# Attention inputs read during layer 3, an earlier overflow flag, and a re-timed attention plan

## The chip, the cores and the metric

The kernel runs on one core of one Trainium2 chip. The metric is the device time of one execution in microseconds. The engines are named as the profile names them: PE (TensorE), DVE (VectorE), ACT (ScalarE), POOL (GpSimd) and SP (SyncE, which here only issues DMAs).

## The reference, cut to what matters

x holds 32 images of 1024 channels and 14 x 14 pixels. Two residual layers follow each other. `_amm` stands for scores against 16 centroids per group, a softmax over the 16, and a product with a table; `_gn` and `_bn` are group and batch norms.

```
x = x + L0(_gn(x)):                     # three table layers
    out = relu(bn1(_amm(x, c1, lut1)))              # 1024 -> 256
    out = relu(bn2(_amm(extract3x3(out), c2, lut2)))  # 256 -> 256
    out = bn3(_amm(out, c3, lut3))                    # 256 -> 1024
    return relu(out + identity)
x = x + L1(_gn(x)):                     # linear attention, 16 heads of 64
    q = elu(Wq x[:512] + bq) + 1;  k = elu(Wk x[512:] + bk) + 1
    qr, kr = rope(q), rope(k);  v = x
    z  = 1 / (q . mean_n(k) + 1e-6)
    kv = s*s * sum_n kr v;   attn = (qr kv) * z
    lepe = depthwise_conv3x3(x, lepe_w) + lepe_b
    return attn + lepe
```

All sums run in float32. bn3 needs the mean and variance of all tokens, so attention can begin only when layer 3 is done.

## The kernel before, in words

Layers 1 to 3 are in `layers` (L419). Layers 1 and 2 go through 16 pairs of images, 8 units a pair (`units`, L543): a unit's scores, exponentials, softmax (DVE transposes, sums, reciprocal, and one POOL product) and the product with its table block on PE, the last one some units behind the first. Layer 3 (L850 to L930) goes through 14 chunks `k` of 448 tokens. For a chunk, PE makes 8 blocks `m` of 128 channels, each out of 8 products with `luts` (L909); ACT copies a block to `o` (L917), DVE takes its statistics (L918), and SP stores `o` to the scratch `o3d` in DRAM (L924). `o` has two buffers. In between, the scores of the next chunk are made (L874, L881) and its softmax. After the last chunk `add_up` sums the softmax denominators, and `bn_final` (L320) turns statistics into scale `sc3` and shift `bi3`.

The exponentials are taken without a maximum. Denominators that overflow are found by a flag: three sums are compared with 1e36 (L940), reduced, summed over partitions by a small PE product (L943), written as an integer `bad` (L945) and loaded into a register of each engine (L946). The branch at L947 repeats the three layers in an exact form if the flag is set, which it is not in the profile.

Attention (from L954) first loads its weights `wk` and `wq` into the eight `lut` buffers (L243), biases, masks and tables (L974 to L998), and derives small tables on DVE (L986 to L1016). The order of everything after that is written by `Plan.write`: each piece of work has an engine, a rank and a weight; the planner runs the pieces in a model, taking on each engine the ready one with the lowest rank, and the instructions are then issued in that order, engine by engine.[...] Buffers belong to slots; a slot's ring is taken in turn.

`pair(p, t)` gives the pieces of one pair of images, `t` being 80 p. For each half of the channels (h=1 for keys, h=0 for queries): `load` takes x and two thirds of `o3d`; `front` scales x into a bank `w` (ACT, L1124), adds layer 0's result and the residual (DVE, L1133, L1138) and takes statistics (L1143); `group_norm` averages on PE (L1165) and ends on POOL; `normalise` writes the padded images `y` (ACT, L1218). `channels` makes 8 key and 8 query products (PE, L1250; ACT, L1259 and L1262; DVE, L1271 or L1267). `rope` turns them on POOL (L1291 to L1298). `tokens` transposes on PE (L1309), `products` makes kv (L1346, L1355), `normalisers` makes z (PE L1397, DVE L1406 and the reciprocal L1407). `normalise_q` spreads z over partitions with a PE product by `hsel` (L1418), an ACT copy `zb` (L1424) and a POOL product (L1421). `attend` puts a channel pair's sums into two banks `pa` (PE, L1438), and `lepe` adds eight taps of the 3 x 3 convolution there one by one (DVE, L1455; the middle tap is in the residual's scale) and then adds `pa` to x (L1469). `store` writes x out (L1478).

Of the kernel before, what the change touches and what calls it, by code (L numbers as in the profile page):

```python
# [10 lines left out]
F32 = mybir.dt.float32  # L11
# [30 lines left out]
class Slot:  # L42


    def __init__(self, pool, make):
        self.pool, self.make, self.ap, self.left = pool, make, None, 0
# [5 lines left out]
class Plan:  # L52
# [9 lines left out]
    def __init__(self, bufs):  # L62
        self.pieces, self.last, self.read = [], {}, {}
        self.ring = {n: [None] * k for n, k in bufs.items()}
# [19 lines left out]
    def write(self):  # L84
# [9 lines left out]
        nexts = {n: 0 for n in self.ring}  # L94
# [7 lines left out]
        def roomy(slots):  # L102
            take = {}
            for s in slots:
                if s.ap is None:
                    ring = self.ring[s.pool]
                    k = take.get(s.pool, nexts[s.pool])
                    old = ring[k % len(ring)]
                    if old is not None and old.left:
                        return False  # L110
                    take[s.pool] = k + 1
            return True

        while events:
            now, _, done = heapq.heappop(events)
            if done is not None:
# [4 lines left out]
                for s in self.pieces[done][5]:  # L121
                    s.left -= 1
            if events and events[0][0] <= now:
                continue
            for e in engines:
# [17 lines left out]
                for s in slots:  # L143
                    if s.ap is None:
                        ring = self.ring[s.pool]
                        ring[nexts[s.pool] % len(ring)] = s
                        nexts[s.pool] += 1
                        s.ap = s.make()
# [12 lines left out]
def conv_preact_kernel(ctx: ExitStack, tc: tile.TileContext, a: dict, out: bass.AP):  # L161
# [78 lines left out]
    def load_lut(name, shape, src, b):  # L240

        t = wts.tile(shape, F32, tag=f"lut{b}", name=f"{name}_{b}")
        nc.sync.dma_start(t, src(b))  # L243
        return t

    def load_luts(name, shape, src):
        return [load_lut(name, shape, src, b) for b in range(8)]
# [72 lines left out]
    def bn_final(pool, stats, i, hs, sc, bi):  # L320
# [4 lines left out]
        mv = pool.tile([P, n, 2], F32, tag=f"mv{hs[0]}", name=f"mv{i}")  # L325
        for k, h in enumerate(hs):
            nc.vector.bn_aggr(mv[:, k, :], stats[:, h].rearrange("p m s -> p (m s)"))
# [80 lines left out]
    lut_rows = lambda t: lambda b: a[t][b * 512 : (b + 1) * 512].rearrange("(s q) w -> q s w", q=P)  # L408
# [5 lines left out]

    sc3 = cp.tile([P, CT], F32, tag="sc3", name="sc3")
# [3 lines left out]
    def layers(exact, sums):  # L419
# [107 lines left out]

        def add_up(layer, n):
# [1088 lines left out]
```

## Time and profile before

| quantity | value |
|---|---|
| time, median of 3 runs | 3925.6 us (3922.6 to 3926.0) |
| the profiled execution | 3921.2 us |
| its span | 3919.2 us |
| PE, DVE, POOL, ACT busy | 95%, 78%, 57%, 42% of the span |
| layer 3's last product ends | 2657.7 us |
| attention's first key product starts | 2712.5 us |
| last pair's first key product starts | 3793.0 us |

The profile is one execution on the chip, and its times count from the start of the span. A row names the line, the engine, the operation and what it writes and reads; in brackets stands how long the engine was idle before, and what ended that. Busy shares say little by themselves here, since layers, passage and attention have different limits; the times of three places are set beside the page in the table.

### The profile page before, as it was taken

Reading aid. Unit: us, or ns where it says so; the run is one execution under the profiler, and the core shown is the slowest. Engines: PE = TensorE matmul, PEld = TensorE weight load, DVE = VectorE, ACT = ScalarE, POOL = GpSimd, SP = SyncE. Lnnn points to the kernel's source line nnn. Section 1 sums busy time; section 2 is a strip of 40 time slices with the busy share of each in tenths; the row PEclk is TensorE's granted clock in tenths of the full one; section 3 lists DMA queues with packets and bytes.
Section 4 is the critical chain, followed back from the end, with each engine's and each line's share of the span. In section 5 each row is a group of like instructions: output and inputs, shape, how many; then the busy total and the mean of one; then the engine's idle time right before and its main releaser. Section 6 shows DMA issues by size and latency. Waiting matters only on the chain. (4 is left out here: it accounts for less than half of the span.)

```text
span 3919.2 us, 45921 instructions
## 1 busy us (share of the span) xinstructions
PE 3741.2 (95%) x16475; PEld 2097.3 (54%) x16475; DVE 3054.1 (78%) x4395; ACT 1664.6 (42%) x3797; POOL 2226.9 (57%) x1248
## 2 busy tenths in 40 slices
PE   8999999999999999999999999994999999999995
PEld 5555555544555455554444444442666666666664
DVE  8999999978888888888533333323799999999997
ACT  4555555533333333333222211213756666666661
POOL 7999999964444444444211111103877777777773
PEclk9999999999999999999999999997999999999997
DMA  3111111024333333432011110114122222222111
GB/s 114 34 34 33 34 33 32 2 74 104 83 69 87 69 83 69 97 73 60 32 38 38 38 38 19 38 38 135 42 67 62 71 71 63 67 71 75 55 54 34
DMA packets 209028, 228.13 MB, mean 58 GB/s; under 512 B 23888, under 2 KB 206672, under 8 KB 208792
## 3 DMA queue, kind: packets, MB, share of 16 engines
q1 hardware_dynamic: 208216, 224.96, 21.4%
q8 instruction: 133, 2.18, 0.2%
q14 instruction: 103, 0.84, 0.1%
q10 hardware_dynamic: 576, 0.15, 0.0%
HBM read 151.51 MB, written 73.55 MB: 57 GB/s over the span
## 5 line engine op out<-in xcount | busy, mean ns | idle before, releaser
L525 POOL TENSOR_TENSOR t<-t,r 128x1664 f32<-128x1664 f32 (+1 forms) x284 | 1064.2, 3747 | 1188.8 <-DVE r L524 1153.1
L558 PE MATMUL po<-t,lut 128*128 128x392 f32 x4096 | 1418.4, 500 | 0.5 <-POOL t L525 0.5
L558 PEld LDWEIGHTS po<-t,lut 128*128 128x128 f32 x4096 | 760.0, 190 | 627.0 <-issue 124.7
L487 ACT ACTIVATE t<-sc,cbias 128x392 f32<-128x392 f32 (+1 forms) x1136 | 579.8, 593 | 1034.8 <-PE sc L823 646.9
L1250 PE MATMUL mm<-y,qk 128*128 128x392 f32 x2048 | 727.1, 507 | 4.1 <-POOL xbi L1192 4.1
L909 PE MATMUL po<-t,lut 128*128 128x448 f32 x1792 | 680.3, 540 | 0.0
L499 DVE STREAM_TRANSPOSE tt<-t 128x1664 f32<-128x1664 f32 (+1 forms) x284 | 544.3, 1917 | 168.5 <-ACT t L487 168.5
L1455 DVE SCALAR_TENSOR_TENSOR pa<-y,lepe_w,pa 128x406 f32<-128x406 f32 x1024 | 607.1, 638 | 10.5 <-PE pa L1438 9.2
L524 DVE STREAM_TRANSPOSE r<-rc 128x1664 f32<-128x1664 f32 (+1 forms) x284 | 546.6, 1925 | 21.3 <-DVE rc L518 0.9
L1250 PEld LDWEIGHTS mm<-y,qk 128*128 128x128 f32 x2048 | 386.5, 194 | 283.9 <-issue 32.8
L909 PEld LDWEIGHTS po<-t,lut 128*128 128x128 f32 x1792 | 338.4, 190 | 339.9 <-issue 339.6
L918 DVE BATCH_NORM_STATS2 stats<-o 128x6 f32<-128x448 f32 x112 | 69.0, 617 | 488.4 <-ACT o L917 488.4
L516 DVE TENSOR_REDUCE sm<-tt 128x104 f32<-128x832 f32 (+2 forms) x284 | 423.1, 1490 | 5.4
L502 POOL TENSOR_TENSOR tt<-tt 128x832 f32<-128x832 f32 x128 | 248.1, 1938 | 7.8 <-DVE tt L499 7.8
L917 ACT COPY o<-po 128x448 f32<-128x448 f32 x112 | 59.0, 528 | 419.6 <-PE po L909 375.5
L518 DVE RECIPROCAL rc<-sm 128x104 f32<-128x104 f32 (+1 forms) x284 | 229.5, 808 | 9.8
L814 PE MATMUL sc<-patch,cw 64*128 64x392 f32 x1024 | 211.1, 520 | 4.7 <-DMA patch<-h1d 3.2
L1291 POOL TENSOR_TENSOR kr<-k,cosq 128x784 f32<-128x784 f32 x64 | 104.0, 1625 | 129.8 <-DVE k L1271 100.6
L1421 POOL TENSOR_TENSOR qr<-qr,zb 128x784 f32<-128x784 f32 x64 | 116.1, 1845 | 103.0 <-ACT zb L1424 103.0
L526 ACT ACTIVATE sm<-sm 128x104 f32<-128x104 f32 (+1 forms) x284 | 86.2, 304 | 174.6 <-DVE rc L518 174.6
L1124 ACT ACTIVATE w<-x,tb,gn_a 128x196 f32<-128x196 f32 x256 | 133.3, 521 | 58.5 <-DMA x<-in_x_dram 33.9
L814 PEld LDWEIGHTS sc<-patch,cw 64*128 64x128 f32 x1024 | 90.5, 186 | 116.5 <-issue 73.4
(156 smaller groups left out, 3844.6 us busy)
## 6 DMA issues: line engine op xcount, KB each, us to landing
patch<-h1d SPq DMA_DIRECT2D x248, 162.8 KB
x<-in_x_dram SPq DMA_DIRECT2D x32, 784.0 KB
o3d<-o SPq DMA_DIRECT2D x14, 1792.0 KB
x<-in_x_dram SPq DMA_DIRECT2D x64, 392.0 KB
o3q<-o3d SPq DMA_DIRECT2D x64, 392.0 KB
out_dram<-x SPq DMA_DIRECT2D x64, 392.0 KB
h1d<-pad SPq DMA_DIRECT2D x96, 225.0 KB
patch<-h1d SPq DMA_DIRECT2D x124, 108.5 KB
```

Source lines behind the costliest of these rows:

```text
L487: nc.scalar.activation(t[:, j, : sc.shape[1]], sc, AF.Identity if exact else AF.Exp, bias=bias[:, j : j + 1],)
L499: nc.vector.transpose(tt, tf)
L502: nc.gpsimd.tensor_tensor(tv[:, :, :8], tv[:, :, :8], tv[:, :, 8:], ALU.add)
L516: nc.vector.tensor_reduce(sm, tv, AX.X, ALU.add)
L518: nc.vector.reciprocal(rc, sm)
L524: nc.vector.transpose(r, bc(rc, 2, KC))
L525: nc.gpsimd.tensor_tensor(tf, tf, r, ALU.mult)
L558: nc.tensor.matmul(po[h], luts[b][:, j, h * P : (h + 1) * P], ts[u % len(ts)][:, j, :N2], start=(b == 0 and j == 0), stop=(b == 7 and j == 3),
L814: nc.tensor.matmul(sc, w8[r, 8 * h + 4 * (j // 2) + g], grid(pbuf[n % NPB][r, j // 2, g]), start=True, stop=False,)
L909: nc.tensor.matmul(po, luts[g][:, m * P : (m + 1) * P], t3[h][:, g % 4, :], start=(g == 0), stop=(g == 7),)
L1250: nc.tensor.matmul(pv(), w[kt][:, m0 : m0 + P], ywin(p, first + kt), start=(kt == 0), stop=(kt == 3),)
L1455: nc.vector.scalar_tensor_tensor(acc, neighbours(p, c, 15 * (k // 3 - 1) + k % 3 - 1), lw[:, c, k : k + 1], acc, ALU.mult, ALU.add,)
```

## The change

In the order of the program:

- The planner's buffers are made once, and a slot takes any free buffer of its kind instead of the next one of a ring. The eight table buffers are one set of tiles for all layers.
- A pool of its own holds attention's inputs. In layer 3, chunk 1 issues their loads (biases, masks, tables, x of the first pair), chunk 2 the loads of the first pair's `o3d` for the key half, chunk 3 derives the small tables. The weights are issued behind the last store of layer 3, ahead of the branch.
- The flag is formed and loaded into registers ahead of chunk 13's products. The aggregates of layer 3 are taken block by block in that chunk.
- Only borders of `y` and gaps of `kr` are set to zero.
- For the first pair, x and the key half's `o3d` are there already, and odd channels of `front` use a `pa` bank.
- For all pairs but the last, z is stored to the DRAM scratch `zd` and read back by four DMAs that repeat four rows over 128 partitions (`keep`, `spread`). The last pair keeps the PE product.
- Of each channel of the key half, one tap leaves DVE: ACT scales the shifted image into `side`, POOL adds it to x. In the last pair three taps of every channel go this way.
- In the last pair the five other taps of six channels are PE products with a diagonal matrix that ACT makes in `wk`'s buffers; they open the bank, and `attend` adds to it. The last two channels keep five taps on DVE.
- All ranks are a table `due`, with other values, and some pieces have `held` and `room` as further dependencies.

Cut to its core (rank table and renamed slots shortened):

```diff
-    def __init__(self, bufs):
+    def __init__(self, tiles):
         self.pieces, self.last, self.read = [], {}, {}
-        self.ring = {n: [None] * k for n, k in bufs.items()}
+        self.free = {n: list(ts) for n, ts in tiles.items()}
...
-            take = {}
-            for s in slots:
-                if s.ap is None:
-                    ring = self.ring[s.pool]
-                    k = take.get(s.pool, nexts[s.pool])
-                    old = ring[k % len(ring)]
-                    if old is not None and old.left:
-                        return False
-                    take[s.pool] = k + 1
-            return True
+            take = [s.pool for s in slots if s.ap is None]
+            return all(take.count(n) <= len(self.free[n]) for n in take)
...
+                    if s.left == 0:
+                        self.free[s.pool].append(s.ap)
...
-    def load_lut(name, shape, src, b):
-        t = wts.tile(shape, F32, tag=f"lut{b}", name=f"{name}_{b}")
-        nc.sync.dma_start(t, src(b))
-        return t
-    def load_luts(name, shape, src):
-        return [load_lut(name, shape, src, b) for b in range(8)]
...
+    def load_lut(b, src):
+        v = weights[b]
+        if len(src.shape) == 3:
+            v = v.rearrange("p (s w) -> p s w", s=src.shape[1])
+        nc.sync.dma_start(v, src)
+        return v
...
+    def bn_sum(mv, stats, h):
+        nc.vector.bn_aggr(mv, stats[:, h].rearrange("p m s -> p (m s)"))
...
+    def attention_inputs(stack):
+        def loads(_):
+            pool = stack.enter_context(tc.tile_pool(name="pre", bufs=1, side="right"))
+            def tile_(name, shape):
+                given[name] = pool.tile(shape, F32, tag=name, name=name)
+                return given[name]
+            for n, k in (("qb", a["qb"]), ("kb", a["kb"].rearrange("o (r j p) -> p (o r) j", p=P, r=2))):
+                nc.sync.dma_start(tile_(n, [P, 2, 4]), k)
+                tile_(n + "u", [P, 2, 4])
+                tile_(n + "d", [P, 2, 4])
+            for n, shape in (("lepe_w", [P, CT, 9]), ("lepe_b", [P, CT]), ("kvmask", [P, 256])):
+                nc.sync.dma_start(tile_(n, shape), a[n])
+            for n in ("cosq", "sinq"):
+                t = tile_(n, [P, 4, 14])
+                v = a[n].rearrange("p j (r c) -> p j r c", c=14)
+                nc.sync.dma_start(t[:, :2], v[:, :2, :, 0])
+                nc.sync.dma_start(t[:, 2:], v[:, 2:, 0, :])
...
+            for h in (1, 0):
+                for i in range(2):
+                    nc.sync.dma_start(
+                        given[f"x{h}"][:, :, i * HW : (i + 1) * HW],
+                        x[i, 4 * h * P : 4 * (h + 1) * P].rearrange("(c q) n -> q c n", q=P),
+                    )
...
+        def tables(ps_tr):
+            g = given
+            for n in ("qb", "kb"):
+                nc.vector.tensor_scalar(g[n + "u"], g[n], 1.0, None, ALU.add)
+                nc.vector.tensor_scalar(g[n + "d"], g[n], -1.0, None, ALU.mult)
...
+            nc.tensor.transpose(ph, g["hp"].rearrange("p j h -> p (j h)"), ident)
+            nc.vector.tensor_copy(g["hsel"], ph)
+        def third(_):
+            for k in range(2):
+                nc.sync.dma_start(given[f"o3_{k}"], o3d[:, 4 + 2 * k : 6 + 2 * k, :N2])
+        def projections(_):
+            for b in range(8):
+                t = a["wkT" if b < 4 else "wqT"]
+                load_lut(b, t[(b % 4) * P : (b % 4 + 1) * P])
+        return [loads, third, tables], projections, [third, projections]
...
+        def overflow(pool):
+            good = pool.tile([P, 1], F32, tag="good", name="good")
+            nc.vector.tensor_scalar(sums, sums, 1e36, None, ALU.is_le)
+            nc.vector.tensor_reduce(good, sums, AX.X, ALU.min)
+            pf = ps_tr.tile([P, 512], F32, tag="tr", name="pf")[:1, :1]
+            nc.tensor.matmul(pf, good, ones[:, :1], start=True, stop=True)
+            bad = pool.tile([1, 1], mybir.dt.int32, tag="bad", name="bad")
+            nc.vector.tensor_scalar(bad, pf, -1.0, float(P), ALU.mult, ALU.add)
+            return nc.values_load(bad[0:1, 0:1], min_val=0, max_val=P)
...
-            for b in range(8):
-                at(8 * (NP - 1) + b, next_lut(b))
+            for b in range(7):
+                at(8 * (NP - 1) + b + 1, next_lut(b))
...
+                elif not more and not exact:
+                    add_up(2, 2 * NCH)
+                    again = overflow(once)
+                if early and k > 0:
+                    early.pop(0)(ps_tr)
...
+                        if not more:
+                            bn_sum(mv3[:, m, :], stats3, m)
...
-            add_up(2, 2 * NCH)
-            bn_final(once, stats3, 3, range(CT), sc3, bi3)
...
+            bn_final(once, None, 3, range(CT), sc3, bi3, mv3)
...
+    early, weights4, repeated = attention_inputs(pre)
     with tc.manual_schedule(engines=engines):
-        layers(False, sums)
-    with ExitStack() as s:
-        fp = s.enter_context(tc.tile_pool(name="flag", bufs=1))
-        fps = s.enter_context(tc.tile_pool(name="ps_flag", bufs=1, space=PSUM))
-        good = fp.tile([P, 1], F32, tag="good", name="good")
-        nc.vector.tensor_scalar(sums, sums, 1e36, None, ALU.is_le)
-        nc.vector.tensor_reduce(good, sums, AX.X, ALU.min)
-        pf = fps.tile([P, 512], F32, tag="pf", name="pf")[:1, :1]
-        nc.tensor.matmul(pf, good, ones[:, :1], start=True, stop=True)
-        bad = fp.tile([1, 1], mybir.dt.int32, tag="bad", name="bad")
-        nc.vector.tensor_scalar(bad, pf, -1.0, float(P), ALU.mult, ALU.add)
-        again = nc.values_load(bad[0:1, 0:1], min_val=0, max_val=P)
+        again = layers(False, early)
+        weights4(None)
...
+            layers(True)
+            for f in repeated:
+                f(None)
...
-            nc.gpsimd.memset(t, 0.0)
+            v = t[:, :, LEAD : LEAD + 2 * IMG]
+            for border in (
+                t[:, :, :LEAD],
+                t[:, :, LEAD + 2 * IMG :],
+                v.rearrange("p c (r m) -> p c r m", m=15)[:, :, :, 14],
+                v.rearrange("p c (i n) -> p c i n", i=2)[:, :, :, 210:],
+            ):
+                nc.gpsimd.memset(border, 0.0)
...
-            xt = slot("x", [P, 4, N2])
+            xt = Slot("x")
+            if p == 0:
+                xt.ap = given[f"x{h}"]
...
-            do(SP, rank - 12, 0.9, quad, (), [(xt, c) for c in range(4)], lag=5.0)
+            if p > 0:
+                do(SP, rank - 12, 0.9, quad, (), [(xt, c) for c in range(4)], lag=5.0)
...
+                if p == 0 and h == 1:
+                    ot.ap = given[f"o3_{k}"]
+                else:
+                    do(SP, rank - 11 + 8 * k, 0.45, third, (), [(ot, 0), (ot, 1)], lag=4.5)
...
-            w = bank("w")
+            w = Slot("pa" if p == 0 and c % 2 else "w")
...
+            held = [("held", j // 2)] if keys else []
+            done = ["wk"] if keys and p == NP - 1 else []
+            do(PE, rank, 2.76, product, ys_ + done, [pq, *held], lag=0.25)
...
+            def keep():
+                nc.sync.dma_start(zd[p % 2], z)
...
+            if p < NP - 1:
+                do(SP, rank - 10, 0.45, keep, ["z"], [("zd", p % 2)], lag=2.5)
...
             def spread():
+                nc.sync.dma_start(zb(), bc(zd[p % 2, 32 * j : 32 * j + 4], 1, 32))
...
+            if p < NP - 1:
+                do(SP, rank - 10, 0.58, spread, [("zd", p % 2)], [zb], lag=5.0 + 1.7 * n)
+            else:
+                do(PE, rank, 0.6, select, ["z"], [pz], lag=0.25)
+                do(ACT, rank - 10, 0.48, lambda: nc.scalar.copy(zb(), pz()[:, :N2]), [pz], [zb])
...
+                                start=(r == 0 and not onto),
+                                stop=(r == 1 and (i == 1 or not onto)),
...
-            for n, k in enumerate([k for k in range(9) if k != 4]):
-                do(DVE, rank + n, 0.555, tap(k), [("y", p % 2, c)], [pa])
-            do(DVE, rank + 8, 0.48, added, [pa], [(xt, c % 4)])
+            for k in mine:
+                do(DVE, rank, 0.545, tap(k), [("y", p % 2, c)], [pa])
+                rank += due["tap"]
...
+            def shifted():
+                off = LEAD + offset(k)
+                v = ys[p % 2][:, c, off : off + 2 * IMG]
+                nc.scalar.activation(
+                    side(),
+                    v.rearrange("p (i r c) -> p i r c", r=15, c=15)[:, :, :14, :14],
+                    AF.Copy,
+                    scale=lw[:, c, k : k + 1],
+                )
+            def onto():
+                nc.gpsimd.tensor_tensor(
+                    xc(), xc(), side().rearrange("p i r c -> p (i r c)"), ALU.add
+                )
+            do(ACT, rank - 6, 0.52, shifted, [("y", p % 2, c)], [side])
+            do(POOL, rank - 4, 1.02, onto, [side], [(xt, c % 4)], port=True)
...
+        diagonals = iter([t[:, P * n : P * n + P] for t in wk for n in range(C // P)])
+        def diagonal_taps(p, c, ks, pa, rank):
+            for n, k in enumerate(ks):
...
+                def diagonal(k=k, dg=dg):
+                    nc.scalar.activation(dg, ident, AF.Copy, scale=lw[:, c, k : k + 1])
+                def piece(n=n, k=k, dg=dg):
+                    nc.tensor.matmul(
+                        pa()[:, :406],
+                        dg,
+                        neighbours(p, c, offset(k)),
+                        start=(n == 0),
+                        stop=False,
+                    )
+                do(ACT, rank, 0.3, diagonal, [], ["wk", ("dg", c, k)])
+                do(PE, rank, 0.68, piece, [("dg", c, k), ("y", p % 2, c)], [pa], lag=0.25)
...
+        due = dict(
+            front_k=-72,
+            front_q=-28,
...
+            key=8.5,
+            rope_k=4.25,
+            query=23,
+            step=7.75,
+            row=4.25,
+            rope_q=55,
...
+            den=60,
+            scaled=45,
+            attend=72.5,
+            sums=20,
+            lepe=86,
...
+            normalisers(p, qs, ks, at["den"] - (10 if p == NP - 1 else 0))
...
+            last = p == NP - 1
+            pools = {0: "pa pa", 1: "mm mm", 2: "pa w", 3: "mm mm"} if last else {}
+            for n, j in enumerate(js):
+                pa = [Slot(b) for b in pools.get(n, "pa pa").split()]
+                by_pe = last and n < 3
+                taps = {}
                 for hp in range(2):
                     c = 2 * j + hp
-                    lepe(p, c, pa[hp], xts[c // 4], t + T + 2.0 + 9.5 * (2 * n + hp))
+                    taps[c] = [k for k in range(9) if k != 4]
+                    for m in range(3 if last else c // 4):
+                        r = at["side"] + due["taps"] * 2 * n + due["half"] * hp
+                        side_tap(p, c, taps[c].pop(1), xts[c // 4], r)
+                    if by_pe:
+                        diagonal_taps(p, c, taps[c], pa[hp], at["diagonal"] + n)
+                        taps[c] = []
```

## Prediction, made before the changed kernel was run

> **What bounds the kernel now.** I read the page's groups and slices first, then busy time by stretch, the waits and the timeline at the three places that the change touches. Times are of the profiled execution: span 3919.2 us, whole execution 3921.2. Layers 1 and 2 keep their instructions and their order in the changed program, so only the end of layer 3, the passage to attention, and attention count.
>
> The passage, TensorE's timeline and the chain of waits:
> ```profile
> 2639.55 18.20 PE L909 MATMUL po<-t,lut 128*128 128x448 f32 x48
> ...
> 2712.48 7.86 PE L1250 MATMUL mm<-y,qk 128*128 128x392 f32 x16 [4.08 <-POOL xbi L1192]
> ```
> ```profile
> 2672.07 4.33 DMA qk<-in_wkT_dram
> 2676.41 4.06 SPq L974
> 2682.02 3.60 SPq L998
> 2689.16 5.10 DMA o3q<-o3d
> 2698.91 7.11 DMA o3q<-o3d
> ```
> Layer 3's last product ends at E = 2639.55 + 18.20 = 2657.75; the first key product starts 54.7 us later. The chain between is loads: flag, branch, weights, tables, then input.
>
> One pair of images in attention (TensorE's timeline) and eight of them (busy time: PE, PEld, DVE, ACT, POOL, clock, DMA):
> ```profile
> 3205.29 3.71 PE L1346 MATMUL mm<-vt,kt 105*64 105x128 f32 x64
> 3210.00 2.48 PE L1418 MATMUL mm<-z,hsel 32*128 32x392 f32 x8 [0.99 <-DVE z L1407]
> 3212.41 7.09 PE L1250 MATMUL mm<-y,qk 128*128 128x392 f32 x16
> ```
> ```profile
> 2930.62:3509.34 578.72, 568.67 (x3519) 384.18 (x3518) 557.30 (x1310) 381.42 (x800) 428.57 (x385) 0.98 0.23 68
> ```
> ```profile
> 3212.00:3215.00 3.00, 3.00 (x6) 1.51 (x5) 3.00 (x7) 1.23 (x3) 3.00 (x2) 0.53 0.14 18
> ```
> A pair takes 578.72/8 = 72.34 us; TensorE is busy 71.1 of it, VectorE 69.7, GpSimd 53.6, ScalarE 47.7. TensorE stops once, for z, and behind that stop its granted clock is 0.53: two products take 6.93 us instead of 5.28. Both engines are near their limit, so one alone made lighter gains little.
>
> The end of the program, VectorE's timeline:
> ```profile
> 3903.66 8.95 DVE L1455 SCALAR_TENSOR_TENSOR pa<-y,lepe_w,pa 128x406 f32<-128x406 f32 x16 [2.12 <-PE pa L1438]
> 3912.52 1.04 DVE L1469 TENSOR_TENSOR x<-pa,x 128x392 f32<-128x392 f32 x2
> ```
> Four such rounds of 12.0 us (attend, 16 taps, two sums) run from 3864.6 with TensorE idle. From the last pair's first product (3793.0) to the end is 126.2 us.
>
> **Part 1, layer 3: +3.4 us.** The flag is formed before chunk 13's products. TensorE waits through the last copy and statistics of chunk 12 (1.24 us by the rows at 2657.75 to 2658.99), three small VectorE operations (0.3), its own small product, `bad` (0.4) and the register load (0.9: `bad` ended at 2664.4, the branches stood at 2665.1 to 2665.7): 2.9. All of chunk 13's products queue behind it, ACT's copies behind those. The mask transpose of chunk 3 waits for ten small VectorE operations, some 1.5 us, partly under a gap that is there anyway (1.3 us before each score): +0.5. Lower end 2, upper 6 if the clock drops. The input loads in chunks 1 and 2 (13 and 2 more DMAs on SP ahead of the store of `o`) cost nothing: the slow small ones hold SP some 10 us, a chunk takes about 87, `o` has two buffers; without that cover the next chunk's copies would wait. The eight aggregates move into chunk 13 under its products, except the last (0.4).
>
> **Part 2, the passage: 54.7 becomes 36.8, -17.9.** After: statistics E+1.2, aggregate +1.6, GpSimd's power and three operations (2.5, as before) E+4.1. Each engine still has its branch: VectorE needed 3.1 us (2665.7 to 2668.8), SP 3.0, TensorE 4.2, TensorE's now right at E. Together at E+8.4, where it was 12.0. Then `tb`, scale, and four channels, now through two kinds of banks: E+17.5. But VectorE's order in the changed program puts the query half's first two sums before the key half's group norm, and TensorE's puts both halves' averages before the first product. That half's `o3d` third is issued on SP behind six loads of x. In front of it in the queue: the last store (1.8 MB, at 230 GB/s until E+8.3), eight weights (4.2 MB at 412 GB/s, as at 2674 to 2682) to E+18.5, x (2.4 MB at 340, as at 2690 to 2706) to E+25.6, itself to E+27.2. The row of 7.11 us, a third behind eight loads of x, shows that these queue. From there VectorE has 9.1 us of sums and statistics (1.56 a channel plus two sets of small operations) and TensorE its average 0.5: E+36.8. Ends: 30 (third not behind x) to 42. The smaller zeroing on GpSimd (9.6 us of 2669.8 to 2679.4) lay under the loads: 0. Moved weights cost nothing as long as they land by E+36.8.
>
> **Part 3, fifteen pairs: 72.04 becomes 68.8, -48.6.** From 2712.48 to 3793.03 is 15 x 72.04. Removed from TensorE per pair: the z products 2.45 (3210.00 to 3212.41), the wait 1.2, the slow clock 1.65: 72.34 - 5.3 = 67.05. From VectorE: four taps, each 8.87/16 = 0.554 (sixteen in a row at 3867.7): 69.66 - 2.2 = 67.46. ScalarE loses four copies (1.9) and gains four scaled shifts (2.1 by the 0.53 of L1262); GpSimd gains four sums at 0.95 (L1295): 57.5. Neither binds. VectorE sets the pair; I add 1.3, since its waits on `e` (12.3 us in eight pairs, 1.5 each) come from product-then-exponential and stay, some of them excepted that follow the slow clock. Floor 67.5, upper end 72.
>
> [...] By the row the drop stands right behind that wait in every pair, while waits of 1.28 us in layer 3 leave the clock at 1.00. I take the row[...].
>
> *z through memory.* z is stored, then read back by four loads that repeat four rows over 128 partitions. SP holds them in order, GpSimd's four `times` wait for them, ropes wait behind these, and TensorE's attend behind `times`. Cover in TensorE's new order: transposes 0.45, kv products 3.71, four key products 10.6: 14.7 us. Needed: z 3.3 + store 3.7 (issue 0.4; store of x ended issue at 3222.1, its reload started 3.3 later) + load 3.7 (x, 2688.2 to 2691.9) + `times` 1.95 = 12.7. So 2 us to spare. [...] anything ahead of it on SP makes TensorE wait. That is the second reason for the 1.3.
>
> **Part 4, the last pair: 126.2 becomes 105, -21.2.** TensorE from its first product: 16 products 42.2, transposes 9, kv 7.4, denominators 1.5, attends of the pair before 6.4, z 2.6, 30 diagonal taps at 0.68 (0.66 for 392 columns) 20.4, own attends 6.3: 95.8. After the third attend (4.3 before that end) VectorE has ten taps and four sums, 7.6, and the store 5.6 (3913.6 to 3919.2). 95.8 - 4.3 + 7.6 + 5.6 = 104.7. GpSimd (ropes 41, `times` 7, 24 side sums 23) is nearly as long, and could add 8. The z wait here is under six diagonal taps (4.1 of 3.3).
>
> **Sum.** +3.4 - 17.9 - 48.6 - 21.2 = -84.3. Against the profiled execution 3921.2 - 84.3 = 3836.9. The median of the runs, 3925.6, is 4.4 above it: forecast 3841.
>
> **Rivals.**
> 1. *TensorE still stops each pair*, at attend instead of z, with the clock drop: 67.05 + 2 + 1.65 = 70.7; +1.9 x 15 = +28, 3870. [...] Against: two by the row.
> 2. *The pair doesn't shorten*: the wait only moves, as GpSimd waited 6.6 us a pair for `zb` (52.8 in eight) and VectorE for `e`. The pair stays 72.04, passage and tail remain: 3841 + 48.6 = 3890.
> 3. *Slower*: z's way through memory ties up GpSimd and attend in each pair. Passage, layer 3 and tail give 35.7, so it must cost 2.4 a pair: 74.4. With the clock drop TensorE has 68.7, so attend must wait 5.7, i.e. store and load take 15.1 us where the cover leaves 9.4. At 20 us a pair is 79.3: 3925.6 + 109 - 35.7 = 3999. Against: nothing of 200 to 400 KB took over 7.2 us here, even behind other loads.
> 4. *More*: at the floors (67.5, passage 30, tail 100): 3841 - 20 - 7 - 5 = 3809.
>
> **Numbers.** Forecast 0.55 (own range 3815 to 3862), rival 1 0.22, rival 2 0.10, rival 3 0.05, rival 4 0.06, no change 0.02. The range 3808 to 3888 leaves out rival 3 and the ends of 2 and 4. No change means within 0.2%, 7.9 us, about what a measurement tells: faster 0.93, same 0.02, slower 0.05.
>
> **What would show it.** First product 36.8 us after layer 3's last; a wait of some 3 us before chunk 13; 68.8 between equal products of neighbouring pairs, no z wait, clock 1.00 there, POOL's wait for `zb` under 7; 105 us from the last pair's first product. It is wrong if attend waits for `qr` on TensorE in each pair, if the clock still falls once a pair, or if GpSimd or VectorE alone holds the last pair.

## The result and the profile after

The changed kernel takes 3862.8 us (median of 4 runs, 3861.7 to 3866.5) against 3925.2 for the kernel before: the ratio is 0.984 (95% interval 0.983 to 0.986), 62 us less. The forecast was 3841, 84 less. Of k_dve below one execution alone counts (3845.2 us): its other one, 4029.3 us, ran in a slower state, at a mean granted clock of 0.92 instead of 0.984. The profiled execution has a span of 3860.0 where it was 3919.2. Stage by stage:

| stage | before | after | difference | forecast |
|---|---|---|---|---|
| layers 1 and 2, to layer 3's first product | 1922.2 | 1919.9 | -2.3 | 0 |
| layer 3, first to last product | 735.6 | 741.4 | +5.9 | +3.4 |
| E, the end of layer 3's last product, to the first key product | 54.7 | 41.7 | -13.0 | -17.9 |
| fifteen pairs | 15 x 72.03 | 15 x 69.31 | -40.8 | -48.6 |
| last pair, from its first product to the end | 126.2 | 117.3 | -9.0 | -21.2 |
| span | 3919.2 | 3860.0 | -59.2 | -84.3 |

The first row has the same instructions in both kernels; over the fourteen profiles of this study layer 3 began between 1919.9 and 1925.6, so a total tells no difference of a few microseconds, and the stages are compared one by one. The fifteen pairs are not alike either: the first, which has no pair ahead of it, takes 60.3 us (68.2 before); pairs three to twelve take 69.98 us each (72.33 before), and only these are steady.

**Layer 3.** TensorE's timeline after, around the flag, and busy time by stretch (PE, PEld, DVE, ACT, POOL busy; then the granted clock, the DMA share, GB/s):

```profile
2609.42 0.19 PE L605 MATMUL pf<-ones,good 128*1 128x1 f32 x2 [1.76 <-DVE good L603]
2611.29 4.94 PE L1005 MATMUL po<-t,lut 128*128 128x448 f32 x8 [1.68 <-issue]
```
```profile
2611.00:2613.00 2.00, 1.71 (x4) 0.89 (x5) 0.00 (x0) 0.00 (x0) 0.00 (x0) 0.90 1.04 381
2613.00:2615.00 2.00, 2.00 (x4) 1.01 (x3) 0.00 (x0) 0.00 (x0) 0.00 (x0) 0.50 0.66 242
2615.00:2617.00 2.00, 2.00 (x5) 0.90 (x4) 0.00 (x0) 0.00 (x0) 0.00 (x0) 0.74 0.00 0
```

The wait is 1.76 + 0.19 + 1.68 = 3.6 us. Behind it the granted clock is 0.50 for 3.4 us, from 2612.6 to 2616.0, which loses 1.7 us (0.2 + 1.0 + 0.5 in the three stretches).

**The passage.** Timeline after (SPq rows are DMAs being issued):

```profile
2661.92 0.53 SPq L1022 DMA_DIRECT2D o3d<-o  x1
...
2662.56 4.33 SPq L237 DMA_DIRECT2D lut<-in_wkT_dram  x4
...
2666.99 3.21 SPq L237 DMA_DIRECT2D lut<-in_wqT_dram  x4
...
2682.18 0.42 DVE L1061 TENSOR_TENSOR tb<-gn_b,bi 128x256 f32<-128x256 f32 x1 [16.53 <-SPq L1036]
...
2686.36 12.34 SPq L1172 DMA_DIRECT2D o<-o3d  x4
...
2693.15 0.63 DVE L1201 SCALAR_TENSOR_TENSOR w<-o,sc,w 128x392 f32<-128x392 f32 x1 [2.49 <-DMA o<-o3d]
...
2703.04 1.66 PE L1318 MATMUL mm<-y,lut 128*128 128x392 f32 x2
```

VectorE stands for 16.5 us at L1036, the branch, although its flag has long been read. The reading that w_late tests below is that the join behind the branch waits here for the weights, which have just been put into the queue. Everything goes on at E + 20.8 (E = 2661.3), not at the forecast's E + 8.4.

**A pair.** z's way through memory, in the timeline after:

```profile
3531.52 0.34 SPq L1481 DMA_DIRECT2D zd<-z  x1
...
3535.69 2.33 SPq L1497 DMA_DIRECT2D zb<-zd  x4
...
3541.13 1.85 POOL L1503 TENSOR_TENSOR qr<-qr,zb 128x784 f32<-128x784 f32 x1 [7.10 <-DMA zb<-zd]
```

From VectorE's first operation on z (3528.31) to GpSimd's first product with it are 12.8 us, 3.2 to make z and 9.6 behind it (forecast 10.7). From 3543 to 3548 us, when by the bytes only loads of `zb` are left, the sixteen engines are busy 0.25 to 0.28 of the time and move 88 to 99 GB/s. In ten pairs TensorE waits 0.5 us for `qr`: this fits under its cover. But TensorE still stops once a pair, in another place: transposes wait for a bank that ACT has yet to copy (`kt`). Two pairs of TensorE's timeline, and the clock behind the second:

```profile
3178.13 0.69 PE L1380 MATMUL mm<-ident,y 128*105 128x128 f32 x4 [1.48 <-ACT kt L1383]
...
3389.60 0.69 PE L1380 MATMUL mm<-ident,y 128*105 128x128 f32 x4 [2.44 <-ACT kt L1383]
```
```profile
3392.00:3394.00 2.00, 2.00 (x5) 1.18 (x5) 2.00 (x6) 1.70 (x5) 0.41 (x1) 0.50 0.63 160
```

**The last pair.** Timeline after of VectorE, GpSimd and TensorE:

```profile
3782.58 8.74 DVE L1450 TENSOR_TENSOR kmm<-ks,hmean 128x32 f32<-128x32 f32 x2
```
```profile
3788.34 0.95 POOL L1366 TENSOR_TENSOR kr<-kr,ru 128x392 f32<-128x392 f32 x1
3789.26 1.00 POOL L1577 TENSOR_TENSOR x<-x,side 128x392 f32<-128x392 f32 x1
3790.23 0.94 POOL L1369 TENSOR_TENSOR kr<-kr,ru 128x392 f32<-128x392 f32 x1
3796.92 1.53 POOL L1362 TENSOR_TENSOR qr<-q,cosq 128x784 f32<-128x784 f32 x1 [5.75 <-DVE q L1335]
```
```profile
3791.91 2.90 PE L1318 MATMUL mm<-y,lut 128*128 128x392 f32 x8 [2.04 <-DVE q L1335]
3796.83 1.87 PE L1380 MATMUL mm<-ident,kr 128*105 128x128 f32 x8 [2.02 <-DVE q L1335]
3799.55 5.02 PE L1318 MATMUL mm<-y,lut 128*128 128x392 f32 x8 [0.85 <-DVE q L1335]
```

A product of 128 x 32 numbers, 0.6 us at most before, holds VectorE 8.7 us. It ends when GpSimd, which had worked without a gap, runs dry at 3791.2. What was issued to VectorE behind it, a `q` first, starts only at 3791.24. TensorE then waits three times, 4.9 us in all, and its product at 3799.55, at a granted clock of 0.57, takes 5.02 where such eight take 2.80.

### The profile page after: what moved, and what is told of

Read it like the earlier page. It is cut to its first block, busy times and chain, and to the rows that moved or that the text cites. A ratio compares the mean times of both kernels' runs of the same rounds, so it can differ in the third digit from the quotient of the medians.

```text
span 3860.0 us, 45872 instructions
## 1 busy us (share of the span) xinstructions
PE 3715.2 (96%) x16415; PEld 2079.6 (54%) x16415; DVE 3002.4 (78%) x4281; ACT 1687.7 (44%) x3851; POOL 2300.7 (60%) x1338
## 5 line engine op out<-in xcount | busy, mean ns | idle before, releaser
L1318 PE MATMUL mm<-y,lut 128*128 128x392 f32 x2048 | 721.7, 500 | 4.8 <-DVE q L1335 2.9
L1540 DVE SCALAR_TENSOR_TENSOR pa<-y,lepe_w,pa 128x406 f32<-128x406 f32 x900 | 540.7, 636 | 17.9 <-PE pa L1522 15.1
L1318 PEld LDWEIGHTS mm<-y,lut 128*128 128x128 f32 x2048 | 375.7, 191 | 257.6 <-issue 14.3
L1503 POOL TENSOR_TENSOR qr<-qr,zb 128x784 f32<-128x784 f32 x64 | 117.6, 1850 | 70.2 <-DMA zb<-zd 68.2
L1327 ACT ACTIVATE e<-mm,kbd 128x392 f32<-128x392 f32 x128 | 74.1, 579 | 170.4 <-PE mm L1318 168.4
```

The lines of the kernel that those rows point to most:

```text
L1318: nc.tensor.matmul(pv(), w[kt][:, m0 : m0 + P], ywin(p, first + kt), start=(kt == 0), stop=(kt == 3),)
L1540: nc.vector.scalar_tensor_tensor(acc, neighbours(p, c, offset(k)), lw[:, c, k : k + 1], acc, ALU.mult, ALU.add,)
```

## The experiments

One thing of the program comes first: the planner goes through the engines in the order of a Python set, which is not fixed from build to build, and two orders of attention come out of that. The rows of the last pair tell which one the profile shows. The experiments fix that one, so each edit can be seen alone, except plan_b, which fixes the other. All results at once, stages as above:

| kernel | median, us | ratio to before | E to first key | a pair | last pair |
|---|---|---|---|---|---|
| the changed kernel | 3862.8 | 0.984 | 41.7 | 69.31 | 117.3 |
| w_late | 3857.2 | 0.983 | 40.1 | 68.90 | 117.6 |
| w_q | 3849.6 | 0.981 | 28.0 | 69.24 | 117.6 |
| w_flag | 3858.1 | 0.984 | 42.6 | 69.10 | 117.5 |
| kmm1 | 3914.4 | 0.998 | 42.7 | 72.51 | 118.9 |
| kmm_ps | 3844.2 | 0.980 | 42.5 | 68.42 | 109.5 |
| plan_b | 3850.3 | 0.981 | 42.0 | 68.63 | 110.2 |
| no_side | 3847.3 | 0.980 | 41.8 | 68.55 | 112.4 |
| z_pe | 3872.0 | 0.987 | 41.4 | 70.58 | 104.9 |
| k_dve (profiled execution) | 3845.2 | | 41.9 | 68.54 | 109.4 |
| best3 | 3826.8 | 0.976 | 29.3 | 68.48 | 111.4 |
| best_ns | 3823.4 | 0.975 | 29.1 | 68.22 | 110.7 |
| split | 3815.4 | 0.973 | 29.4 | 68.15 | 105.4 |

Intervals of the ratios are 0.0016 to 0.002 to either side (kmm1 0.0009). Layer 3 takes 741.4 us in all of them, but 735.8 where the flag is formed late (w_flag, best3, best_ns, split). In w_late, w_flag, w_q and the changed kernel the pairs have the same instructions in the same order; that they still take 68.90 to 69.31 us is mostly the clock, which stands at half for 3.4 us once, three times, four times and four times in their fifteen pairs. Each time loses 1.7 us, 0.11 a pair in this table.

**Weights behind the branch (w_late).**

```diff
         again = layers(False, early)
-        weights4(None)
...
     with ExitStack() as s:
...
+        weights4(None)
         wk, wq = weights[:4], weights[4:]
```


> The eight weight loads are issued behind the branch instead of ahead of it; every other instruction keeps its order. Theory A: the join behind the branch waits for every DMA that is outstanding, so in the changed kernel it waited for 4.2 MB of weights, and the engines went on 20.8 us after layer 3's last product. With the weights behind the join they go on after about 8.4 to 9 us; weights, x and the query half's o3d third then queue as the prediction had them, and the first key product stands 36 to 38.5 us after layer 3's last (41.7 in the changed kernel): 3 to 6 us less in all, about 3858. Theory B: the join is late for another reason (SP's own 7.5 us of issuing weights[...]), and the loads now start only then: first product 46 to 50 us after layer 3's last, 3868 to 3871.

Timeline of w_late:

```profile
2673.99 0.42 DVE L1061 TENSOR_TENSOR tb<-gn_b,bi 128x256 f32<-128x256 f32 x1 [5.10 <-DVEq L1035]
...
2675.06 1.97 SPq L237 DMA_DIRECT2D lut<-in_wqT_dram  x4
...
2677.20 10.36 SPq L1157 DMA_DIRECT2D x<-in_x_dram  x6
...
2687.66 12.62 SPq L1172 DMA_DIRECT2D o<-o3d  x4
...
2694.74 0.63 DVE L1201 SCALAR_TENSOR_TENSOR w<-o,sc,w 128x392 f32<-128x392 f32 x1 [12.26 <-DMA o<-o3d]
```

With E = 2664.6, `tb` starts at E + 9.4 instead of E + 20.8: theory A's reading of the join holds. (SP's own 7.5 us of issuing, of theory B, are less than the 11.4 us won.) But only 1.7 us arrive at the first product. What was won is waited off 20 us later, for the query half's third: SP needs 10.4 us to issue six loads of x behind the weights, and the third is issued behind them, from 2687.7 on.

**That third first (w_q).**

```diff
...
+        own = [once.tile([P, 2, N2], F32, tag=f"o3q{k}", name=f"o3q{k}") for k in range(2)]
+        for k in range(2):
+            nc.sync.dma_start(own[k], o3d[:, 2 * k : 2 * k + 2, :N2])
         weights4(None)
...
```


> As the kernel with the weights behind the branch (first key product 40.05 us after layer 3's last, VectorE waiting 12.3 us for the query half's o3d third). Now that third has two tiles of its own and is issued ahead of the weights; every engine keeps its order. Theory A: what held the passage since the join is freed is this third, queued behind weights and x. Then VectorE's wait of 12.3 us goes to under 1 and the first product stands 27 to 30 us after layer 3's last: 10 to 13 us less, about 3846. Theory B: the weights take its place (they land some 12 to 14 us after VectorE goes on, i.e. 22 to 24 us after layer 3's last, and may be slower behind the third): first product 31 to 36. Theory C: the queue was not the reason: within 2 us of 40.

```profile
2672.93 0.91 SPq L1054 DMA_DIRECT2D o3q<-o3d  x2
...
2673.38 0.42 DVE L1064 TENSOR_TENSOR tb<-gn_b,bi 128x256 f32<-128x256 f32 x1 [5.08 <-DVEq L1035]
...
2692.02 2.31 PE L1324 MATMUL mm<-y,lut 128*128 128x392 f32 x3
```

In w_q's timeline (E = 2664.0) the first key product stands at E + 28.0. Theory A: 12 us came from the order in one queue, with no byte less. The total shows 7.6 of them, since the clock fell three times more in w_q's pairs (5.1 us).

**The flag late again (w_flag).** w_late, with `again = overflow(once)` moved from chunk 13 to behind `bn_final`.

> As the kernel with the weights behind the branch, and in addition the overflow flag is formed where it was before the change: after layer 3's last products instead of ahead of chunk 13's. Theory A (the prediction's numbers): layer 3 ends 2.9 us earlier, the engines stand together 12 us after its end instead of 8.4, so the two cancel: within 1 us of the kernel with the weights alone moved. Theory B: the register loads and branches hide behind the last store, which lands some 8.3 us after the last product anyway: then only the 2.9 us in layer 3 show, and this kernel is 3 us faster. Theory C: the early flag is worth more than it costs: 3 us or more slower.

Layer 3 is 5.6 us shorter, the passage 2.6 longer: no theory had both sizes, B is nearest (3.0 us ahead by these stages). By the stages the early flag costs more than it saves. The totals don't show it: the medians differ by less than they scatter, and w_flag has two more half-clock stretches in its pairs.

**kmm in another form (kmm1).**

```diff
-                    nc.vector.tensor_tensor(
-                        kmm[i].rearrange("p r j h -> p (r j) h")[:, :, :4],
-                        bc(ks()[:, :, :, i].rearrange("p r j -> p (r j)"), 2, 4),
-                        bc(hmean, 1, 8),
-                        ALU.mult,
-                    )
+                    for h in range(4):
+                        nc.vector.tensor_scalar(
+                            kmm[i].rearrange("p r j h -> p (r j) h")[:, :, h],
+                            ks()[:, :, :, i].rearrange("p r j -> p (r j)"),
+                            hmean[:, h : h + 1],
+                            None,
+                            ALU.mult,
+                        )
```


> The small product kmm = ks * hmean, which has two operands in SBUF, is made by four tensor_scalar operations each (one operand from SBUF, the other a value per partition); order as before, every other instruction the same. Theory A: in the last pair VectorE stood 8.6 us in kmm because GpSimd worked without a gap until 3791.2[...]. Then kmm takes about 1 us in all there, TensorE's three stops behind it (2.04, 2.02, 0.85 us) and the slow product (5.02 for 2.80) go, and the last pair shrinks from 117 to 110 to 113 us; the other fifteen pairs change by less than 0.3 us each. In all 4 to 7 us less, about 3857. Theory B: VectorE waited there for something else (ks, a load): kmm still ends at the same place, no change within 1 us. Theory C: GpSimd's chain sets the last pair's length: kmm is short, but the pair stays within 1.5 us of 117.

All three theories missed: 52 us slower. The tile's row in kmm1 (least, median and longest ns):

```profile
L1451 DVE TENSOR_SCALAR kmm<-ks,hmean x128: 210/225/8618, 2742.3 to 3842.6; 128x8 f32<-128x8 f32 x128
```

The 8.6 us stay, now with one SBUF operand and a value per partition, and a pair takes 72.51 us where it took 69.31. That these instructions, too, wait for GpSimd is a reading of the durations; it was not shown.

**kmm with an operand in PSUM (kmm_ps).**

```diff
+        hm = tiles["w"][0][:, 480:484]
+        nc.vector.tensor_copy(hm, hmean)
...
-                        bc(hmean, 1, 8),
+                        bc(hm, 1, 8),
```


> The changed kernel with one operand of kmm = ks * hmean in PSUM instead of SBUF (hmean is copied once into unused columns of bank w): still two instructions a pair, order the same. [...] Theory A: an instruction of VectorE with one operand in PSUM doesn't wait for GpSimd (the group norm's gq<-gst,mm takes 0.175 us in the changed kernel where gq<-gst,gd took 0.476 before): kmm takes under 0.3 us each, TensorE's stops in the last pair (2.04, 2.02, 0.85) and its slow product (5.02) go, the last pair is 109 to 112 us instead of 117; total about 7 less, 3856. Theory B: what makes VectorE wait is the write of kmm to SBUF, not the read: kmm stays at 8.6 in the last pair, no change.

```profile
L1452 DVE TENSOR_TENSOR kmm<-ks,w x32: 173/178/188, 2741.9 to 3770.9; 128x32 f32<-128x32 f32 x32
```

No instance of the tile's row takes longer than 0.188 us any more (what kmm takes beyond that elsewhere is called its wait), and the last pair is 7.8 us shorter, as theory A had it. Beyond it, each other pair is 0.9 shorter: kmm had also waited up to 1.6 us there, TensorE's stop was longer (16.5 us in ten pairs, 13.6 in kmm_ps), and the clock fell four times (6.8 of these 13.4 us), in kmm_ps never.

**The planner's other order (plan_b).**

> The changed kernel as it is, but the planner looks at GpSimd before VectorE when both can start at the same time (which of the two comes first was left open in the changed program). All instructions are the same, only attention's order differs in places; the last pair makes kmm late, behind VectorE's taps. Theory A: the pair's length is set by the resources, not by such details: pairs of 69.4 us as in the changed kernel within 0.3, passage the same, last pair 110 to 117 since kmm falls into another place: 3853 to 3866. Theory B: the order of a few waiting pieces decides (TensorE's stop for kt is such a detail): pairs differ by 0.5 us or more, total by more than 8 us either way.

```profile
L1450 DVE TENSOR_TENSOR kmm<-ks,hmean x32: 176/184/1994, 2774.4 to 3813.1; 128x32 f32<-128x32 f32 x32
```

12.5 us faster: 0.7 a pair, as B said, and 7.0 in the last pair. There kmm comes late (at 3811.1) and takes at most 2.0 us in all its 32 instances. Pairs and last pair are within 0.8 us of kmm_ps's, so the detail that decides is probably where kmm falls; that was not tried by itself.

**No side taps (no_side).**

```diff
-                    for m in range(3 if last else c // 4):
+                    for m in range(3 if last else 0):
```


> In pairs 0 to 14 no tap goes by ACT and GpSimd: all eight taps of every channel stay on VectorE (the last pair keeps its side taps); the planner writes a new order. Theory A (the prediction's): VectorE, 66.7 us busy in a pair of 69.3 to 70, gets four taps of 0.554 back and sets the pair: 70.3 to 71.5, 15 to 33 us more in all. Theory B: TensorE's one stop a pair, 1.7 us for kt (ACT's copy), is there because ACT carries the shifted images; without them it goes and the pair takes 67.6 to 68.5: 10 to 25 us less.

Busy time over ten pairs, kmm_ps and no_side:

```profile
2850.00:3550.00 700.00, 685.11 (x4352) 465.47 (x4350) 675.40 (x1618) 486.67 (x1012) 583.25 (x532) 1.00 0.30 85
```
```profile
2850.00:3550.00 700.00, 683.44 (x4344) 462.77 (x4343) 692.03 (x1651) 464.93 (x964) 541.44 (x486) 1.00 0.29 84
```

VectorE got its four taps back and is busy 98.9% of the time, yet the pair takes 68.55, less than the changed kernel's 69.31. So VectorE did not set the pair there, against the prediction's A. In pairs three to twelve (69.10 us each in kmm_ps, 69.44 here) TensorE works 67.6 us in the one and 67.8 in the other. Its stop for `kt` falls from 16.5 us in these ten pairs (changed kernel; 13.6 in kmm_ps) to 6.0, as B said; in its place come stops of 3.6 for VectorE's `k`, 3.1 for `qr` and 2.4 for `nmc`, so here VectorE is close to binding too. The side taps bought nothing in these pairs; best3 and best_ns below, both free of kmm's wait, say the same (68.48 with them, 68.22 without).

**z on TensorE again (z_pe).** `select` and the copy `zb` in all pairs, no `zd`.

> In every pair z is spread over partitions by the PE product and ACT's copy, as before the change, instead of through memory; everything else as in the changed kernel, in a new order of the planner. Theory A (the prediction's): per pair TensorE gets back 2.45 us of products, and some or all of the wait for z (1.2) and the slow clock behind it (1.65): pairs of 71.6 to 74.3 instead of 69.3, 35 to 75 us more. Theory B: the way through memory gave nothing, since TensorE now waits 1.7 us a pair for kt instead: pairs of 70.3 at most, under 15 us more.

```profile
3330.53 0.68 PE L1380 MATMUL mm<-ident,y 128*105 128x128 f32 x4 [0.77 <-ACT kt L1383]
...
3332.16 1.72 PE L1498 MATMUL mm<-z,hsel 32*128 32x392 f32 x8
...
3764.03 2.88 PE L1318 MATMUL mm<-y,lut 128*128 128x392 f32 x8
```

The last row is the last pair's first key product. Pairs take 70.58, 0.3 above B's limit; the total is up by 9, under its 15, because the last pair is 12.3 shorter in this order. Kmm takes at most 1.0 us in it; kmm_ps gained 7.8 there by kmm alone, and the rest is not traced. Against kmm_ps (68.42), which has no kmm wait, the pair is 2.2 longer. In the last ten whole pairs, where both are steady, it is 1.7 (70.64 to 68.95), and z's products there take 1.75: they explain it, though kmm still waits up to 1.6 us in z_pe. In these ten pairs there is no stop for z and no slow clock, though z is spread as it was before the change. The prediction credited 2.45 + 1.2 + 1.65 a pair to the way through memory. Of the 3.6 from before (72.03) to kmm_ps, 2.2 at most are from that way, and the rest comes from the new order of the work.

**No diagonals (k_dve).** kmm_ps with `by_pe = False`.

> As the kernel with kmm's operand in PSUM (last pair 109.5 us), but without diagonal products: the five taps of six channels of the last pair go back to VectorE, in that pair only; the side taps stay, order else as it was. Theory A (the prediction's): the products with diagonals shorten the last pair, since VectorE's four rounds (attend, ten taps, two sums) then stand one after the other: at 8.2 us each from about 3804 the last sum ends at 3837, 1.5 us later than now (3835.3), and up to 8 us later if the rounds start later or their attends don't overlap: last pair 111 to 118. Theory B: with two sets of banks attend lies under the taps, VectorE needs 6.6 us a round from 3806 on, and TensorE is free of 20 us of products which had VectorE idle for 8.5, 8.3 and 2.0 us: last pair 107 to 110, so the diagonals brought nothing here; the side taps and the order brought the gain.

109.4 as with diagonals: theory B. In kmm_ps VectorE's timeline shows who paid for them:

```profile
3815.43 1.04 DVE L1556 TENSOR_TENSOR x<-pa,x 128x392 f32<-128x392 f32 x2 [8.50 <-PE pa L1524]
3824.78 1.04 DVE L1556 TENSOR_TENSOR x<-mm,x 128x392 f32<-128x392 f32 x2 [8.31 <-PE mm L1524]
```

In k_dve it waits at most 1.3 us for TensorE from 3800 on. The taps were moved from one engine to the other, not shared between them.

**Together (best3, best_ns, split).** best3 is w_q, the late flag and kmm_ps; best_ns leaves out the side taps too; split has in addition `by_pe = last and n == 3`, one round of four on TensorE.

> Four of the tried edits together, with attention's order as in the changed kernel: weights behind the branch, the query half's o3d third with tiles of its own ahead of them, the overflow flag behind layer 3 as before the change, and kmm's operand in PSUM. If the parts add: layer 3 is 5.6 us shorter (its first to its last product took 735.3 us with the flag late and 740.9 with the flag early), the first key product stands about 30.6 us after layer 3's last (28.0 with the early flag, plus 2.6 as the late flag cost with the weights alone moved), pairs 68.4, last pair 109.5: 17.5 us below the 3844.2 of the kernel with kmm's operand alone, about 3827 (3823 to 3831). Rival: the late flag costs more now, since nothing else holds the passage: first product at 33 or later, 3830 or more.

> The same four edits, and in addition no side taps in pairs 0 to 14 (a new order of the planner). Theory A: TensorE alone sets the pair: its work is 67.0 us, the rest are stops; with VectorE 98.9% busy without side taps the pair took 68.55 although kmm still waited up to 1.8 us for GpSimd; free of that it takes 67.8 to 68.5, and the total is within 9 us of the kernel with side taps, rather below it. Theory B: now that kmm no longer waits, VectorE is what is short: 68.7 or more, 5 us or more above.

> As the five edits together (pairs 68.2, last pair 110.7 us), but of the last pair's four rounds only the last takes its five taps a channel as products with diagonals, instead of the first three; nothing changes before the last pair. With all on TensorE (three rounds) the last pair took 109.45, with none 109.44. Theory A: these two are the same length by chance of two different bounds, TensorE with 20 us of diagonal products or VectorE with 22 us of taps after the first attend; with one round on TensorE (6.8 us, in VectorE's first rounds) VectorE has three rounds of 6.6 and two sums: the last pair takes 103 to 107, the total 3816 to 3820. Theory B: something common to both sets its length (attends waiting for GpSimd's last products with z, kv's blocks, the store): 109 to 112, the total within 2 us of 3823.4.

3826.8: the parts add as expected, the first product being at E + 29.3 and the last pair 2 us longer. best_ns stays within A (68.22 a pair); its 3.4 us are less than can be told apart. split brings the last pair to 105.4 and the total to 3815.4, 47 us below the changed kernel. So the equal lengths with and without diagonals were two different bounds, TensorE's and VectorE's, that happened to be equal.

## Why the prediction was right or wrong

The direction and the stated range were right; of the size, a quarter was missing. The result is 0.8 us outside the range given for the forecast itself (3815 to 3862) and nearer to rival 1's 3870 than to 3841, but rival 1's cause, attend waiting for `qr`, was not there. The order of the parts was not right: the last pair was to bring more than the passage, and brought less. Step by step:

- **Layer 3, +3.4: mis-sized, +5.9.** The term "2.9" for the flag measured 5.6 (741.4 less 735.8): 3.6 of wait (1.76 ahead of the flag's product where 1.54 was put, 1.68 behind it where 1.3 was put) and 1.7 of half clock, which the prediction kept as its upper end. The small rest is not traced.
- **"Together at E+8.4": failed.** It counted each engine's branch, but not that the weights hold the join: with them ahead of it the engines went on at E + 20.8, without them at E + 9.4 (w_late). "Moved weights cost nothing as long as they land by E+36.8" is wrong for the same reason. The next step, the third queued behind weights and x, was right in kind: in w_late it held the first product at E + 40.1 (36.8 foreseen), out of that queue E + 28.0 (30 foreseen as the lower end).
- **Pairs, 68.8: a steady pair was mis-sized by 1.2, and what sets it was wrong.** The forecast started from a steady pair (72.34), and such a pair came to 69.98. The mean of 69.31 is nearer by luck: the first pair shrank by 7.9 us, which no step foresaw. The new order puts more of a pair's work behind the next pair's first product, so part of this is paid back in the last pair. TensorE's floor of 67.05 measured 67.6 (kmm_ps, where the clock stays full). "VectorE sets the pair" fell with no_side; the 1.3 added for its waits stood, by chance, where TensorE stops 1.4 to 1.7 us a pair for `kt`. 0.9 are kmm's wait and the half clock that came with it (69.98 with, 69.10 without). z's way through memory took 12.8 where 10.7 was counted, and fits, since 17.3 us passed on TensorE from the denominators' products to attend (3543.86 in the pair shown) where 14.7 was counted; 1.5 of them are the stop for `kt`.
- **The clock drop, read from the row: held in part.** The drop stood behind the z wait in six of the eight pairs of the row, not in every one, as the prediction read it. Rival 1, a stop with the clock drop, came true in four pairs and in another place. Taking the row was right in that half clock does stand behind stops as short as 0.99 us (before) and 2.44 us (after), wrong in that z_pe loses the drop although z stays on TensorE. What decides whether the clock falls behind a stop was not shown (last section).
- **Last pair, 105: failed by 12.** 7.8 are kmm, whose two operands in SBUF the prediction never looked at; kmm_ps shows them. By the rows, another 4.3 are the previous pair's transposes and kv products (0.60 + 3.71), which still run after the last pair's first product and were left out of the 95.8. 104.7 + 7.8 + 4.3 = 116.8, measured 117.3. That diagonals shorten this pair was wrong as made (k_dve).

Left open: which part of the new order took the z stop and its slow clock away, and what would end the stop for `kt`.

## What to carry to other kernels

A load issued early is worth its place only if nothing behind it waits for it too soon: with the weights ahead of the join VectorE went on at E + 20.8, with them behind it at E + 9.4, and with the third ahead of them in the queue the first product stood at E + 28.0 instead of E + 40.1. So look what the next join waits for, and put into the queue first what is needed first. Before taking work off an engine that is 96% busy, ask whether it is the one that sets the period, and after moving it, whether the other engine now stands where the first one did; sharing it can beat both. A tiny VectorE instruction with all its operands in SBUF, next to a GpSimd that never rests, can cost more than a large one: kmm, 128 x 32, took 8.6 us where a sum of 128 x 392 takes 0.56. And before a difference of a few microseconds between two variants is explained, count their half-clock stretches: w_q had three more than w_late with the same order of work.

## What the hardware showed that was not expected

- **A small VectorE product stood through a whole row of GpSimd instructions.** In the last pair eight GpSimd instructions ran end to end from 3781.6 to 3791.2; the first of the two kmm, with both operands in SBUF, took 8.64 us from 3782.6 on. With one operand in PSUM it takes 0.188 us at the longest in 32 instructions (kmm_ps). That GpSimd held it up is a reading of these times; how it did was not shown.
- **Of two stops of nearly one length, one had half clock behind it and one had not.** In the fifteen pairs of the changed kernel the granted clock is at half four times, for 3.41 us each. Two of its stops for `kt`, each as a stretch of 3.41 us that holds most of it and the stretch behind:

```profile
3387.41:3390.82 3.41, 1.22 (x10) 1.21 (x11) 3.38 (x3) 3.33 (x7) 3.41 (x5) 1.00 0.00 0
3390.82:3394.23 3.41, 3.41 (x12) 2.46 (x12) 3.41 (x10) 3.04 (x7) 1.12 (x2) 0.50 0.49 140
3738.98:3742.39 3.41, 1.60 (x13) 1.58 (x14) 3.38 (x5) 3.38 (x8) 3.41 (x4) 1.00 0.00 0
3742.39:3745.80 3.41, 3.41 (x17) 2.25 (x16) 3.41 (x9) 3.38 (x8) 1.58 (x3) 1.00 0.20 63
```

The first stop is 2.44 us long, and behind it the clock is 0.50. The second is 2.47 us long, and the clock stays at 1.00. Before the change a stop of 0.99 us for z, which ended at 3210.0, had half clock behind it from 3212.2 to 3215.6. So the length of a stop alone doesn't tell in these traces; what does was not shown.
